# Graph network on one core: TensorE takes each batch's first product one batch earlier, ahead of the second group of sums

## The chip, the cores and the metric

The kernel runs on one core of one Trainium2 chip. The metric is device microseconds of one execution of the whole program. Ten executions of the kernel before took a median of 3623.09 us, with a lowest of 3620.8 and a highest of 3625.99.

## The reference

There are 6250 nodes with 16 features each and 200000 edges, sorted by destination. Two graph layers follow one another, each with a residual and a layer norm. The change touches only the second:

```python
w_m = (efeat @ W_msg + b_msg).reshape(E, in_f, -1)       # 16 x 16 per edge
w_a = (efeat @ W_attn + b_attn).reshape(E, in_f, -1)
h_src = feat[src][:, :, None]
e1 = w_m * h_src
e2 = w_a * h_src
seg_max = jax.ops.segment_max(e2, dst, num_segments=N)
ex = jnp.exp(e2 - seg_max[dst])
denom = jax.ops.segment_sum(ex, dst, num_segments=N)
attn = ex / denom[dst]
ft = jax.ops.segment_sum(e1 * attn, dst, num_segments=N)
return ft.sum(axis=1)
```

For every edge, then, two 16 x 16 matrices come out of a small product with the edge's 16 attributes; both are multiplied by the source node's features; one goes through a softmax over all edges of the same destination; and the other, weighted by it, is summed by destination.

## The kernel before

**First layer and node update.** Up to about 1620 us the kernel works through the first layer's edges and updates the nodes (lines up to 556). The change leaves that part as it is.

**Second layer.** The edges are cut into four stretches, and a batch takes 256 edges of each: `u` from 0 to 3 names the stretch, 128 edges in two columns. There are `NQ` = 197 batches. Inside `tc.manual_schedule(engines=ORDERED)` the instructions of TensorE, VectorE, ScalarE and GpSimd stand in each engine's queue exactly in the order in which the Python code issues them, and every engine works its queue in order. An instruction that waits holds up all that is behind it on its engine. SyncE's queue is not in `ORDERED`.

The steps of batch `b`, each a helper in the code:

- `gather(b)` (L584): GpSimd issues eight indirect DMAs, one of 128 rows each, which fetch the source nodes' features into `hb`. It is called two batches ahead (`LEAD` = 2).
- `load(b)` (L597): two DMAs from SyncE's queue bring the edge attributes into one of four buffers `ev`.
- `multiply(b, u)` (L611): four TensorE matmuls, attributes by weights, into a PSUM tile `pw`: a half for attention, a half for the message. The pool `psw` has three such tiles, used in turn. Counted through all batches, product number n takes the tile of product n - 3, and so waits until that one's last reader is done.
- `maxima(b, u)` (L623, VectorE): the attention half times the node features, to `xs`, and the largest value by row to `cm`.
- `exps(b, u)` (L629, ScalarE): the exponential of that, in place, less a reference value `neg`.
- `message(b, u)` (L634, VectorE): the message half times the node features, in place in PSUM.
- `product(b, u)` (L638, VectorE): message times exponential, to `xs`. It is the last reader of the tile `pw`.
- `highest`, `across`, `top`, `spread`, `refer` (L653, L656, L662 and L664, L667, L671): the batch's largest value is carried over the partitions by a TensorE transpose, a VectorE reduction, a TensorE matmul with a row of ones and a ScalarE copy, all through one PSUM tile `bank`, to serve as the reference of a later batch.
- `add(b, 0)` and `add(b, 1)` (L688): the two groups of sums by destination, each four matmuls with the 0/1 matrix `oh` into the single PSUM tile `acc`. They are issued in the turn of batch `b + 1`. The second group begins with one matmul (L686) that carries over the sums of the batch before.
- `leave(b)` (L694, ScalarE) copies the finished `acc` to `sums`; `invert(b)` (L699, L700) takes logarithm and exponential of it and writes to `bank`; `fold(b)` (L705, L707, VectorE) multiplies and reduces; and SyncE's queue writes the rows out (L713). They are issued in the turn of batch `b + 2`.

Because TensorE's queue is in order, its work in the turn of batch `b` before the change was: product 0, `across`, products 1 and 2, the first group of sums, `spread`, product 3, the second group of sums. On VectorE the turn runs: `maxima` 0, `message` 0, `maxima` 1, `top`, `message` 1, `product` 0, `maxima` 2, `message` 2, `product` 1, `maxima` 3, `message` 3, `product` 2, `fold`, `highest`, `product` 3. On ScalarE: `leave`, `exps` 0, `invert`, `exps` 1, three of the eight steps of `hot`, `exps` 2, `refer`, `carry`, three steps of `hot`, `exps` 3, the rest of `hot`. In the turns of batches 12, 14 and 16 VectorE also has a check of the input's order and range behind its own work.

Of the kernel before, what the change touches and what calls it, by code (L numbers as in the profile page):

```python
# [43 lines left out]
def gnn_kernel(ctx, tc, x_q, x_t4, src_p, dst_p, src_w, dst_w, prev_w, dst_r, base_h, src_q, dst_q, base_q, ea8_w, ea16, ea16_t,  # L44
# [5 lines left out]
    NQ = base_q.shape[1] // S  # L50
# [67 lines left out]
    with ExitStack() as l0:  # L118
# [166 lines left out]
        def message(b):  # L285
            v = got[b]
            pr = wp.tile([W, G, 16, 8], F32, name="pr")
            nc.vector.tensor_tensor(pr, v["pm"].rearrange("p t (h j) -> p t h j", j=8),
                                    v["ea"].unsqueeze(2).to_broadcast([W, G, 16, 8]), OP.mult)
            v["ms"] = wp.tile([W, G, 16], F32, name="ms")  # L290
            nc.vector.tensor_reduce(v["ms"], pr, AX.X, OP.add)
# [267 lines left out]
    with ExitStack() as l1:  # L559
# [17 lines left out]
        def gather(b):  # L577

            st[b] = {"hb": []}
            for u in range(G // 2):  # L580
                hb = hp.tile([W, 2, D], F32, name="hb")
                for k in range(2):
                    t = b * G + 2 * u + k
                    nc.gpsimd.indirect_dma_start(  # L584
                        out=hb[:, k, :], out_offset=None, in_=x1_dram[:, :],
                        in_offset=bass.IndirectOffsetOnAxis(ap=srcq[:, t:t + 1], axis=0))
                st[b]["hb"].append(hb)

        def load(b):
            ev = evs[b % 4]  # L590
            if b < NQ - 1:
                part = eas_dram.rearrange("r (s n) -> r s n", s=S)[:, :, b * 2 * W:(b + 1) * 2 * W]
            else:
                part = eas_dram[:, EP // S:].rearrange("r (s n) -> r s n", s=S - 1)[:, :, 0:2 * W]
            for r in (0, 32):
                to = ev[r:r + 32, :].bitcast(F32)
                nc.sync.dma_start(out=to.rearrange("r (s n) -> r s n", s=S)[:, 0:part.shape[1], :], in_=part)  # L597
                if b == NQ - 1:
                    nc.sync.dma_start(out=to[:, (S - 1) * 2 * W:], in_=end_dram)
            st[b]["ev"] = ev  # L600
            st[b]["xs"] = xp.tile([W, S, 2, 2, 256], F32, name="xs")
            st.pop(b - 6, None)

        def multiply(b, u):

            v = st[b]
            v[u] = pw = psw.tile([W, 2, 2, 256], F32, name="pw")
            for c in range(2):
                for k in range(2):
                    t = 2 * u + k  # L610
                    nc.tensor.matmul(pw[:, c, k, :], v["ev"][:, t * W:(t + 1) * W], w1[:, c * 256:(c + 1) * 256],  # L611
                                     start=True, stop=True)
# [7 lines left out]
        def maxima(b, u):  # L620

            v = st[b]
            nc.vector.tensor_tensor_reduce(  # L623
                over(v["xs"][:, u, 0]), over(v[u][:, 0]), rows(b, u),
                1.0, -2.0 * BIG, OP.mult, OP.max, cm[:, b * S + u:b * S + u + 1])

        def exps(b, u):
            x = st[b]["xs"][:, u, 0]
            nc.scalar.activation(x, x, AF.Exp, bias=neg[:, b:b + 1])  # L629
# [6 lines left out]
        def product(b, u):  # L636
            x = st[b]["xs"]
            nc.vector.tensor_tensor(x[:, u, 1], st[b][u][:, 1], x[:, u, 0], OP.mult)  # L638
# [12 lines left out]
        def highest(b):  # L651
            st[b]["m1"] = wp.tile([W, 1], F32, name="m1")
            nc.vector.tensor_reduce(st[b]["m1"], cm[:, b * S:(b + 1) * S], AX.X, OP.max)  # L653

        def across(b):
            nc.tensor.transpose(bank[0:1, 0:W], st[b]["m1"], ident)  # L656

        def top(b):

            before = st[b - 1]["top"] if b > 0 else None  # L660
            st[b]["top"] = wp.tile([1, 1], F32, name="top")
            nc.vector.tensor_reduce(st[b]["top"], bank[0:1, 0:W], AX.X, OP.max)  # L662
            if before is not None:
                nc.vector.tensor_tensor(st[b]["top"], st[b]["top"], before, OP.max)  # L664

        def spread(b):
            nc.tensor.matmul(bank[:, W:W + 1], ones_row, st[b]["top"], start=True, stop=True)  # L667

        def refer(b):

            nc.scalar.activation(neg[:, b:b + 1], bank[:, W:W + 1], AF.Copy, scale=-1.0)  # L671
# [8 lines left out]
        def add(b, k):  # L680

            v = st[b]
            if k == 0:
                v["acc"] = pss.tile([W, 512], F32, name="acc")
            elif b > 0:
                nc.tensor.matmul(v["acc"], cols[b % 3], st[b - 1]["sums"], start=False, stop=False)  # L686
            for s in range(S):
                nc.tensor.matmul(v["acc"][s * R:(s + 1) * R, :], v["oh"][:, 2 * s + k, :], v["xs"][:, s, :, k, :],  # L688
                                 start=k == 0, stop=k == 1)

        def leave(b):
            v = st[b]
            v["sums"] = wp.tile([W, 512], F32, name="sums")
            nc.scalar.activation(v["sums"], v["acc"], AF.Copy)  # L694

        def invert(b):
            v = st[b]
            r = wp.tile([W, 256], F32, name="r")
            nc.scalar.activation(r, v["sums"][:, 0:256], AF.Ln, bias=tiny_t)  # L699
            nc.scalar.activation(bank[:, 256:512], r, AF.Exp, scale=-1.0, accum_out=rsum[:, b:b + 1])  # L700
# [40 lines left out]
        with tc.issue_after(tables.ins):  # L741
            for b in range(LEAD):
                gather(b)
            load(0)
            with tc.manual_schedule(engines=ORDERED):
                for u in range(4):
                    multiply(0, u)
                    maxima(0, u)
                highest(0)
                across(0)  # L750
                top(0)
                spread(0)
                refer(0)
                refer(1)
                for b in range(NQ + 2):
                    new, old, gone = b < NQ, 1 <= b <= NQ, b >= 2
                    trail = old and b + 1 < NQ
                    if b + LEAD < NQ:
                        gather(b + LEAD)
                    if b + 1 < NQ:  # L760
                        load(b + 1)
                    if new:
                        multiply(b, 0)
                    if gone:
                        leave(b - 2)
                    if trail:
                        across(b - 1)
                    if new:
                        maxima(b, 0)
                        exps(b, 0)  # L770
                        message(b, 0)
                        multiply(b, 1)
                    if gone:
                        invert(b - 2)
                    if new:
                        maxima(b, 1)
                        exps(b, 1)
                    if trail:
                        top(b - 1)
                    if new:  # L780
                        message(b, 1)
                        multiply(b, 2)
                        product(b, 0)
                    if old:
                        add(b - 1, 0)
                    if trail:
                        spread(b - 1)
                    if new:
                        hot(b, 0, 3)
                        maxima(b, 2)  # L790
                        exps(b, 2)
                        message(b, 2)
                        product(b, 1)
                        multiply(b, 3)
                    if trail:
                        refer(b + 1)
                    if b + 1 < NQ:
                        carry(b + 1)
                    if new:
                        hot(b, 3, 6)  # L800
                        maxima(b, 3)
                        exps(b, 3)
                        message(b, 3)
                        product(b, 2)
                        hot(b, 6, G)
                    if old:
                        add(b - 1, 1)
                    if gone:
                        fold(b - 2)
                    if new:  # L810
                        highest(b)
                        product(b, 3)
                    if b in checks:
                        checks[b]()
                    if b == NQ:
                        clear()
                        far_off()
# [370 lines left out]
```

## Time and profile before

| | |
|---|---|
| median of ten executions | 3623.09 us |
| the profiled execution's own time | 3621.96 us |
| its span, first to last instruction | 3620.2 us |
| instructions | 58991 |
| busy: PE, DVE, ACT, POOL | 3169.0, 3259.6, 2789.5, 1879.7 us |
| second layer, first to last `highest` (L653) | 1620.2 to 3586.2 us |
| first and last gather issued (L584) | 1608.0 and 3579.0 us |
| mean granted TensorE clock over the execution | 0.772 |

PE is TensorE, DVE VectorE, ACT ScalarE, POOL GpSimd and SPq SyncE's DMA queue. A row of the profile names a line, an engine, an operation and `out<-in` by tile names. PEclk is the share of full clock that TensorE was granted. A matmul of 32-bit floats can be shown as two instructions. In the timeline a row gives the start, the length, and in brackets the idle time of that engine just before with what ended it.

### The profile page before, as it was taken

What the parts mean: (1) busy time and instruction counts of PE and PEld (TensorE: products, weight loads), DVE (VectorE), ACT (ScalarE), POOL (GpSimd) and SP (SyncE); (2) the same over time, 40 slices, a digit from 0 to 9 for tenths busy, and PEclk for the clock granted to TensorE, in tenths of its full rate; (3) what the DMA queues carried; (4) which work ended last, traced back from release to release, by engine and by line L of the source; (5) the groups of instructions that cost most, each with busy time, mean ns of one, the idle gap of its engine ahead of it and who ended that gap; (6) DMA issues with size and microseconds to landing.
All of it is one profiled execution on the core that took longest, in us unless ns stands there. A gap on an engine that the chain in (4) does not pass through costs nothing.

```text
span 3620.2 us, 58991 instructions
## 1 busy us (share of the span) xinstructions
PE 3169.0 (88%) x15309; PEld 2221.5 (61%) x15309; DVE 3259.6 (90%) x6470; ACT 2789.5 (77%) x5393; POOL 1879.7 (52%) x1790
## 2 busy tenths in 40 slices
PE   3999999999999999948799999999998998888896
PEld 3999999999999998834344444444444444344343
DVE  5999999999999999879999999999998899898887
ACT  4999999999999999817677777677777676677664
POOL 0222222222222222317777777777777777777774
PEclk9999999999999999956666556666666567766655
DMA  6333333333333333221111111111111111111111
GB/s 182 132 123 123 114 123 119 122 114 123 123 119 118 123 123 118 99 55 37 31 35 35 35 36 36 34 35 35 35 36 36 34 36 35 35 35 35 34 35 25
DMA packets 272706, 263.36 MB, mean 73 GB/s; under 512 B 94437, under 2 KB 233254, under 8 KB 272363
## 3 DMA queue, kind: packets, MB, share of 16 engines
q1 hardware_dynamic: 220187, 240.08, 21.4%
q0 software_dynamic: 50432, 13.01, 3.5%
q10 hardware_dynamic: 1744, 6.41, 0.6%
q8 instruction: 128, 2.10, 0.2%
q14 instruction: 215, 1.76, 0.2%
HBM read 222.08 MB, written 37.05 MB: 72 GB/s over the span
## 4 chain that ended last, share of the span: by engine, by line
PE 51%; DVE 18%; ACT 16%; issue 8%; DMA 6%; POOL 1%; SPq 0%; DVEq 0%; ACTq 0%; POOLq 0%
PE acc L348 20%; PE pw L611 11%; PE acc L688 10%; ACT away L306 6%; DVE xs L638 5%; ACT oba L308 5%; PE acc L686 5%; DVE xs L623 4%; PE pm L283 3%; DMA ev<-eas_dram 3%; DVE pw L634 2%; ACT bank L700 2%; ACT r L699 1%; DMA hb<-x_dram,srcq 1%; PE bank L667 1%
## 5 line engine op out<-in xcount | busy, mean ns | idle before, releaser
L584 POOL DMA_INDIRECT hb<-x_dram,srcq x1576 | 1491.8, 947 | 554.8 <-issue 270.7
L329 POOL TENSOR_TENSOR ll<-oa,sl 128x1024 fp32r<-128x1024 f32 x196 | 380.0, 1939 | 1144.5 <-DVE sl L336 1088.8
L629 ACT ACTIVATE xs<-xs,neg 128x512 f32<-128x512 f32 x788 | 562.9, 714 | 487.6 <-DVE cm L623 486.1
L611 PEld LDWEIGHTS pw<-w,ev 66*128 66x128 f32 x3168 | 613.3, 274 | 408.2 <-issue 300.5
L611 PE MATMUL pw<-w,ev 66*128 66x256 f32 x3168 | 742.1, 391 | 91.0 <-DVE xs L638 71.8
L306 ACT ACTIVATE away<-iota,nsb 128x784 f32<-128x784 f32 x784 | 699.2, 939 | 6.0 <-DVE nsb L184 0.6
L688 PE MATMUL acc<-xs,oh 128*32 128x512 f32 x3152 | 671.4, 939 | 0.7 <-ACT sums L694 0.7
L623 DVE CUSTOM_DVE_ANT_1 xs<-pw,hb 128x512 f32<-128x512 f32 x792 | 537.9, 679 | 88.8 <-PE pw L611 65.1
L308 ACT ACTIVATE oba<-away,one_t 128x3136 fp32r<-128x3136 f32 x196 | 572.8, 2922 | 6.4
L634 DVE TENSOR_TENSOR pw<-pw,hb 128x512 f32<-128x512 f32 x788 | 547.0, 694 | 20.5
L638 DVE TENSOR_TENSOR xs<-pw,xs 128x512 f32<-128x512 f32 x788 | 533.3, 677 | 0.0
L316 DVE TENSOR_SCALAR obd<-iota,sb 128x784 fp32r<-128x784 f32 x784 | 454.6, 622 | 0.0
L646 ACT ACTIVATE away<-iota,nrw 128x32 f32<-128x32 f32 x1576 | 389.6, 306 | 0.0
L348 PE MATMUL acc<-obd,ll 128*128 128x392 f32 x1568 | 347.5, 367 | 0.0
L686 PE MATMUL acc<-sums,col 128*128 128x512 f32 x392 | 329.7, 939 | 0.0
L348 PE MATMUL acc<-oba,ll 128*128 128x392 f32 x1568 | 325.9, 352 | 0.0
L348 PE MATMUL acc<-obd,lh 128*128 128x392 f32 x1568 | 312.8, 341 | 1.0 <-DVE lh L329 1.0
L283 PE MATMUL pm<-tw,ot 128*128 128x128 f32 x1568 | 215.0, 282 | 112.0 <-issue 89.0
L348 PE MATMUL acc<-oba,lh 128*128 128x392 f32 x1568 | 312.9, 341 | 0.0
L667 PEld LDWEIGHTS bank<-top,ones_row 1*128 1x128 f32 x392 | 84.0, 265 | 357.4 <-ACT xs L629 215.0
L348 PEld LDWEIGHTS acc<-oba,ll 128*128 128x128 f32 x1568 | 298.7, 198 | 0.0
L283 PEld LDWEIGHTS pm<-tw,ot 128*128 128x128 f32 x1568 | 207.3, 200 | 138.8 <-issue 135.1
(149 smaller groups left out, 3558.8 us busy)
## 6 DMA issues: line engine op xcount, KB each, us to landing
db<-in_dst_r SPq DMA_DIRECT2D x196, 512.0 KB
ev<-eas_dram SPq DMA_DIRECT2D x392, 128.0 KB
hb<-x_dram,srcq POOLq DMA_INDIRECT x1576
tw<-xw_dram SPq DMA_DIRECT2D x784, 32.0 KB
er<-in_ea_t SPq DMA_DIRECT2D x28, 448.0 KB
eas_dram<-eh SPq DMA_DIRECT2D x28, 448.0 KB
eas_dram<-el SPq DMA_DIRECT2D x28, 448.0 KB
tab_dram<-ft SPq DMA_DIRECT2D x784, 2.0 KB
```

The source lines that it names most:

```text
L283: nc.tensor.matmul(pm[:, t, :], v["ot"][:, t, :], v["tw"][:, 2 * t // G, :], start=True, stop=True)
L306: nc.scalar.activation(v["away"][:, t, :], iota, AF.Abs, bias=nsb[:, b * G + t:b * G + t + 1])
L308: nc.scalar.activation(v["oba"], v["away"], AF.Relu, bias=one_t, scale=-1.0)
L348: nc.tensor.matmul(acc[:, s, :B // 2], l[:, t].rearrange("p a h -> p (a h)"), ob[:, s * B // 2:(s + 1) * B // 2], start=b == 0 and t == GA ...
L584: nc.gpsimd.indirect_dma_start(out=hb[:, k, :], out_offset=None, in_=x1_dram[:, :], in_offset=bass.IndirectOffsetOnAxis(ap=srcq[:, t:t + 1 ...
L611: nc.tensor.matmul(pw[:, c, k, :], v["ev"][:, t * W:(t + 1) * W], w1[:, c * 256:(c + 1) * 256], start=True, stop=True)
L623: nc.vector.tensor_tensor_reduce(over(v["xs"][:, u, 0]), over(v[u][:, 0]), rows(b, u), 1.0, -2.0 * BIG, OP.mult, OP.max, cm[:, b * S + u:b ...
L629: nc.scalar.activation(x, x, AF.Exp, bias=neg[:, b:b + 1])
L634: nc.vector.tensor_tensor(m, m, rows(b, u), OP.mult)
L638: nc.vector.tensor_tensor(x[:, u, 1], st[b][u][:, 1], x[:, u, 0], OP.mult)
L686: nc.tensor.matmul(v["acc"], cols[b % 3], st[b - 1]["sums"], start=False, stop=False)
L688: nc.tensor.matmul(v["acc"][s * R:(s + 1) * R, :], v["oh"][:, 2 * s + k, :], v["xs"][:, s, :, k, :], start=k == 0, stop=k == 1)
```

## The change

TensorE's products are moved. Product 0 of batch `b + 1` is issued in the turn of batch `b`, right after product 3 of `b` and in front of the second group of sums. Product 1 takes the place that product 0 had at the start of the turn, and product 2 stands alone between `across` and the first group of sums. Batch 0 issues its own product 0 at the start. Nothing else is moved, and no instruction is added or taken away; the order on VectorE, ScalarE, GpSimd and SyncE's queue stays as it was.

```diff
                     if b + 1 < NQ:
                         load(b + 1)
+                    if b == 0:
+                        multiply(0, 0)
                     if new:
-                        multiply(b, 0)
+                        multiply(b, 1)
                     if gone:
                         leave(b - 2)
                     if trail:
                         across(b - 1)
                     if new:
                         maxima(b, 0)
                         exps(b, 0)
                         message(b, 0)
-                        multiply(b, 1)
...
                         product(b, 1)
                         multiply(b, 3)
+                    if b + 1 < NQ:
+                        multiply(b + 1, 0)
                     if trail:
                         refer(b + 1)
```

TensorE's work in a turn is then: product 1, `across`, product 2, the first group of sums, `spread`, product 3, product 0 of the next batch, the second group of sums.

## The prediction

> **What bounds the kernel now.** The page first. The changed lines lie in the second layer, the right half of the slices, where the clock falls to 5 to 7 tenths and the chain that ended last is mostly TensorE.
>
> ```profile
> PEclk9999999999999999956666556666666567766655
> PE 51%; DVE 18%; ACT 16%; issue 8%; DMA 6%; POOL 1%; SPq 0%; DVEq 0%; ACTq 0%; POOLq 0%
> L584 POOL DMA_INDIRECT hb<-x_dram,srcq x1576 | 1491.8, 947 | 554.8 <-issue 270.7
> ```
>
> The third line is a second bound that the chain hides: 947 ns and 0.30 us between two issues make 1.25 us, eight times a batch 10.0 us. The loop takes 1966.0 us for 197 batches (L653, 1620.2 to 3586.2), 9.98 us each. In GpSimd's timeline the gathers follow each other from 1608.0 to 3579.0 with only some 4.5 us of longer gaps, at the check batches. The loop cannot outrun them.
>
> Next the distance from each L653 to the next. Two lengths recur, 10.19 and 9.47 us; between 1825.8 and 3005.9 the mean is 9.92, a mix of 62 to 38. In a 10.19 us batch the chain of waits is TensorE alone:
>
> ```profile
> 2414.62 0.51 PE bank L667 x2
> 2415.13 1.16 PE pw L611 x4
> 2416.29 1.71 PE acc L686 x2
> 2418.00 1.87 PE acc L688 x8
> 2419.86 1.15 PE pw L611 x4
> 2421.02 0.21 PE bank L656
> 2421.23 1.71 PE pw L611 x8
> 2422.94 1.87 PE acc L688 x8
> ```
>
> These eight sum to 10.19: `spread`, product 3, second group (two lines), product 0, `across`, products 1 and 2, first group. In a 9.47 us batch the second group is about 1 us per line instead of 1.8, TensorE waits, and VectorE is full but for 0.40 us before `top`. What separates the two is the clock. The busy time in stretches of 3.413 us, laid where the clock switches, shows how it is granted (it switches only at multiples of 3.413 us):
>
> ```profile
> 2455.82:2459.23 3.41, 3.41 (x11) 1.56 (x14) 3.34 (x8) 2.81 (x10) 2.50 (x3) 0.50 0.22 49
> 2459.23:2462.65 3.42, 3.34 (x29) 1.79 (x21) 3.35 (x9) 2.15 (x6) 2.81 (x3) 1.00 0.21 44
> 2462.65:2466.06 3.41, 1.48 (x11) 1.04 (x8) 2.94 (x9) 2.29 (x8) 2.50 (x4) 1.00 0.09 8
> 2466.06:2469.47 3.41, 3.41 (x11) 0.28 (x10) 3.34 (x8) 3.31 (x11) 2.50 (x4) 0.50 0.28 82
> 2472.89:2476.30 3.41, 1.84 (x8) 1.07 (x8) 3.22 (x8) 2.29 (x8) 2.72 (x3) 1.00 0.10 15
> ```
>
> After length, columns 2 to 6 are PE, PEld, DVE, ACT, POOL busy; then the clock. A stretch full of TensorE work without `spread` or `across` (2455.82, 2466.06) is followed by full clock; one half empty (1.48 or 1.84 of 3.41) by half clock. Full stretches that hold a `spread` or an `across` stay at half (2452.41 to 2455.82 does, with `spread` at 2455.31).
>
> **The change part by part.**
>
> *TensorE's work.* The same 4 products, 8 sums, 1 carry, `across` and `spread` per batch: 10.19 us at half clock, no gain.
>
> *Removed.* `maxima` 0 no longer waits for product 0: the 0.64 us before L623 in half-clock batches goes. VectorE had that slack under TensorE's 10.19, so nothing is gained by it; `top` still waits for L700.
>
> *Products 1 and 2.* Product 1 needs `product` 2 of the batch before, ended 2418.81, a microsecond before TensorE gets there: 0. Product 2 now follows `across` directly and needs `product` 3 (starts 0.07 after `highest`, lasts 0.68). At half clock product 1 and `across` cover it (1.15 + 0.21). At full clock it waits some 0.3 us, under the 1.09 us for which `spread` waits anyway. Without that cover it would be 0.3 us a batch.
>
> *Product 0 earlier.* Its `ev` buffer was filled long before: the refill is issued at 2406.13, just as product 3 of the batch that used it ends, and there are four buffers. Cost 0. No queue of SyncE or GpSimd is passed.
>
> *The added wait.* Product 0 of the next batch is fourth after product 1 of this one, so it waits for `product` 1 on VectorE. Behind it in TensorE's queue stands the second group; for that waits `leave`, behind it on ScalarE `exps` 0 and `invert`, and for L700 waits `top`, ahead of everything that leads to `product` 1. That is a ring. Before, the second group stood behind product 3, which needs only `product` 0, 1.91 us earlier (2414.29 against 2416.20). The rows of the ring at half clock:
>
> ```profile
> 2409.74 0.60 ACT L694 ACTIVATE sums<-acc 128x512 f32<-128x512 f32 x1 [0.69 <-PE acc L688]
> 2411.60 0.72 ACT L629 ACTIVATE xs<-xs,neg 128x512 f32<-128x512 f32 x1 [1.26 <-DVE cm L623]
> 2412.23 0.49 ACT L699 ACTIVATE r<-sums,tiny_t 128x256 f32<-128x256 f32 x1
> 2412.75 0.39 ACT L700 ACTIVATE bank<-r 128x256 f32<-128x256 f32 x1
> 2413.30 0.28 DVE L662 TENSOR_REDUCE top<-bank 1x1 f32<-1x128 f32 x1 [0.40 <-ACT bank L700]
> 2416.20 0.68 DVE L638 TENSOR_TENSOR xs<-pw,xs 128x512 f32<-128x512 f32 x1
> ```
>
> Start to start: second group to L694 2.00 (2417.93 to 2419.93); L694 to `exps` 0, if that need not wait, 0.51 to 0.60 (overlapped or not); to L699 0.63; to L700 0.52; to `top` 0.55; to `product` 1 2.90; its length 0.68; to a matmul that waited for it 0.15 (2465.19 to 2465.34); product 0 before L686 0.99 (2415.10 to 2416.09); L686 before L688 1.84. Sum 10.77 to 10.86: **10.8 us** at half clock against TensorE's 10.19; before, 1.91 shorter, the ring was hidden under these. At full clock the TensorE terms shrink to about 1.05, 0.55 and 0.96, and the ring is 8.6, under VectorE's 9.47: no change there.
>
> *How often each clock.* This the trace before cannot show for the new order; bounds are all full clock (the gathers' 10.0 a batch) and all half clock (10.8). Between them: at half clock the clean run without `spread` or `across` is product 0, second group, product 1, again 1.15 + 1.71 + 1.87 + 1.16 = 5.89 us, so a 3.41 us stretch fits inside for about 2.5 of 3.41 positions. Before, 10.19 is nearly three stretches (10.24): the position moved 0.05 a batch, and a bad one lasted 58 us. At 10.8 it moves 0.56, and a bad one is passed in two or three batches. At 9.47 it moves 0.77 the other way, and full clock soon ends: in the batch around 2473 the first group ends at 2472.53 and `product` 1 starts at 2475.91, so the waited-for product 0 would start at 2475.91 + 0.68 + 0.15 = 2476.74, and TensorE has 0.35 + 0.71 us of work in those 4.2. The two drifts balance where the mean is three stretches, 10.24 us, with 0.77 / (0.56 + 0.77) = 58% long batches. With the old 62% it would be 10.30. I take 10.24, the nearest to the switching rows.
>
> *Against a page's rule.* The Trainium skill, "TensorE: Matmul & The Clock Gate", Part 1 and "HAM oscillation", says that only gaps beyond about 3 us in TensorE's work make the clock fall. Here it fell after stretches with 1.48 and 1.84 us of work, none with such a gap. By the page the full clock would hold, and the time would be the gathers', about 3623.
>
> **The sum.** 197 x 10.24 = 2017.3. The three check batches (14.87, 13.99, 13.24) are VectorE's and stay: 42.1 - 3 x 10.24 = +11.4. The first two (9.95, 7.88) stay: -2.6. Together 2026.1 against 1966.0: +60. The span goes from 3620.2 to 3680; the profiled execution's 3621.96 is 1.1 below the median of 3623.09, so I forecast 3683.
>
> **The rivals.** *Not slower: the gathers still decide.* If half-clock batches fall below (10.01 - 9.47) / (10.8 - 9.47) = 41%, the ring hides under 10.0 us of gathers. For it: the faster drift. Against: the emptier full-clock batch. Time 3618 to 3626; it can gain no more than the 4.5 us of gaps, so a gain beyond 0.2% (7.2 us, about what can be measured) is almost excluded. Chance 0.10, and 0.03 for a real gain.
>
> *The wait is hidden, and the change does nothing.* VectorE, freed of 0.64 us, runs ahead, and `product` 1 is done when TensorE arrives. That needs the ring to be 0.6 us shorter than its rows; `top` behind L700 speaks against it. Time 3623, chance 0.05.
>
> *Half clock throughout.* With an idle gap in each batch, full stretches become rare. 197 x (10.8 - 10.24) = 110 more: 3793. Against: the clean run is as long as before. Chance 0.06.
>
> **The numbers.** Forecast 0.76, its own range 3655 (mean 10.10) to 3712 (10.39). For 8 in 10 the low end must reach into the two unchanged cases: 3624 to 3712. Faster 0.03, same 0.14, slower 0.83.
>
> **What would show it.** Right: rows of L611 with an idle of about 0.6 us <-L638 just before L686; `leave` later; L653 distances of 9.5 and 10.7 to 10.9, mean near 10.24; gathers with gaps that VectorE ends. Wrong: distances of 10.19 still there (no ring), a mean of 10.0 with gathers back to back (gathers decide), or a clock of 0.5 throughout.

## The result, and the profile after

The changed kernel takes 3680.41 us (median of 8 runs, 3679.17 to 3681.66), the kernel before, beside it, 3622.31 us: a ratio of 1.0159, with an interval of 1.015 to 1.0168. It is 58 us slower. The profiled execution has a span of 3677.1 us. From the first to the last `highest` (L653) it takes 1619.1 to 3642.0, that is 2022.9 us, where it took 1966.0.

First the page: the clock, the shares of the chain that ended last, and two groups (instructions and their busy time and mean, then the idle time before them and what ended most of it).

```profile
PEclk9999999999999999857777777777777777777776
ACT 39%; PE 26%; DVE 17%; issue 10%; DMA 7%; POOL 0%; SPq 0%; DVEq 0%; ACTq 0%; POOLq 0%
L623 DVE CUSTOM_DVE_ANT_1 xs<-pw,hb 128x512 f32<-128x512 f32 x792 | 538.2, 680 | 146.2 <-PE pw L611 137.2
L694 ACT ACTIVATE sums<-acc 128x512 f32<-128x512 f32 x197 | 117.7, 597 | 344.9 <-PE acc L688 344.9
```

Before the change the group of `leave` read:

```profile
L694 ACT ACTIVATE sums<-acc 128x512 f32<-128x512 f32 x197 | 116.5, 591 | 76.8 <-PE acc L688 72.3 <-issue 2.1
```

The granted clock has risen from 5 to 7 tenths to a steady 7, while the kernel has become slower. The shares of the chain must not be read as a picture of the second layer: they cover the whole execution. ScalarE's rise from 16% to 39% is mostly the first layer's (L306 and L308, 6% and 5% before, 17% and 13% now), and TensorE's fall from 51% to 26% is mostly the 20% that it had there before, at L348. The change leaves these lines as they are; the chain only takes another way through them. For the same reason the 51% before do not say that TensorE bounds the second layer; the rows of one batch do that. The last line is of the second layer: `leave` waited 72.3 us in all for the second group of sums, and waits 344.9 now. That is the wait which the prediction foretold, not the price of it.

Next the chain of waits through one long batch (start, length, engine, tile and line).

```profile
2410.90 1.19 PE pw L611 x4
2412.09 1.71 PE acc L686 x2
2413.80 1.91 PE acc L688 x8
...
2415.73 0.60 ACT sums L694
2416.33 0.61 ACT xs L629
2416.94 0.41 ACT r L699
...
2417.37 0.52 ACT bank L700 x2
...
2417.91 0.29 DVE top L662
```

This is the ring that the prediction wrote down: product 0 of the next batch, the carry, the second group, `leave`, `exps` 0, `invert`, `top`. From `top` it goes on over VectorE's turn to `product` 1 at 2420.82, and from there to the next product 0 at 2421.60. In the timeline of the same batch (start, length, then in brackets the idle time before and what ended it) the joints can be read:

```profile
2410.12 0.68 DVE L638 TENSOR_TENSOR xs<-pw,xs 128x512 f32<-128x512 f32 x1
2410.90 1.19 PE L611 MATMUL pw<-w,ev 66*128 66x256 f32 x4 [1.25 <-issue]
2415.73 0.60 ACT L694 ACTIVATE sums<-acc 128x512 f32<-128x512 f32 x1 [2.57 <-PE acc L688]
2416.86 0.69 DVE L623 CUSTOM_DVE_ANT_1 xs<-pw,hb 128x512 f32<-128x512 f32 x1 [1.18 <-PE pw L611]
```

Product 0 starts 0.10 us after the end of `product` 1 (2410.12 + 0.68 = 2410.80); the profile puts its 1.25 us of idle time down to "issue", but that is the instant at which its tile came free. `leave` then waits 2.57 us. In the fourth row `maxima` 1 waits 1.18 us for product 1, which now stands where product 0 stood.

From batch 20 on, the 177 distances from one L653 to the next are 9.46 us (65 of them) and 10.64 to 10.75 us (109, mean 10.70); the length of 10.19 is gone. The mean is 10.23; before it was 9.95 over the same batches.

What separates the two lengths is the clock under a part of the ring, from the start of product 0 to the start of `leave`. Two such stretches, one of a short batch and one of a long (window, its length, busy PE, PEld, DVE, ACT, POOL with their counts, clock, DMA share, GB/s):

```profile
2401.44:2404.08 2.64, 2.64 (x15) 1.04 (x16) 2.57 (x6) 2.24 (x9) 1.89 (x2) 1.00 0.39 106
2410.90:2415.73 4.83, 4.83 (x15) 1.66 (x15) 4.67 (x11) 2.23 (x8) 3.61 (x5) 0.50 0.24 64
```

Taken from each product 0 to the next, from batch 21 on, all 109 long distances had this stretch wholly at half clock, and all 64 short ones had it wholly at full clock.

### The profile page after: what moved, and what is told of

Same layout as the page of the kernel before. It is cut to its first block, busy times and chain, and to the rows that moved or that the text cites. A ratio compares the mean times of both kernels' runs of the same rounds, so it can differ in the third digit from the quotient of the medians.

```text
span 3677.1 us, 58991 instructions
## 1 busy us (share of the span) xinstructions
PE 3015.1 (82%) x15309; PEld 2143.9 (58%) x15309; DVE 3260.3 (89%) x6470; ACT 2780.2 (76%) x5393; POOL 1880.2 (51%) x1790
## 4 chain that ended last, share of the span: by engine, by line
ACT 39%; PE 26%; DVE 17%; issue 10%; DMA 7%; POOL 0%; SPq 0%; DVEq 0%; ACTq 0%; POOLq 0%
ACT away L306 17%; ACT oba L308 13%; PE pw L611 11%; PE acc L688 8%; PE acc L686 6%; DVE xs L638 5%; DMA ev<-eas_dram 5%; DVE pw L634 3%; ACT bank L700 2%; ACT r L699 2%; DVE xs L623 1%; DVE top L662 1%; ACT sm L296 1%; ACT xs L629 1%; ACT sums L694 1%
## 5 line engine op out<-in xcount | busy, mean ns | idle before, releaser
L611 PE MATMUL pw<-w,ev 66*128 66x256 f32 x3168 | 722.9, 368 | 345.8 <-issue 186.4
L611 PEld LDWEIGHTS pw<-w,ev 66*128 66x128 f32 x3168 | 565.2, 248 | 697.3 <-issue 483.3
L306 ACT ACTIVATE away<-iota,nsb 128x784 f32<-128x784 f32 x784 | 699.2, 939 | 5.9 <-DVE nsb L184 0.5
L623 DVE CUSTOM_DVE_ANT_1 xs<-pw,hb 128x512 f32<-128x512 f32 x792 | 538.2, 680 | 146.2 <-PE pw L611 137.2
L308 ACT ACTIVATE oba<-away,one_t 128x3136 fp32r<-128x3136 f32 x196 | 572.7, 2922 | 6.4
L688 PE MATMUL acc<-xs,oh 128*32 128x512 f32 x3152 | 567.3, 801 | 0.7 <-ACT sums L694 0.7
L634 DVE TENSOR_TENSOR pw<-pw,hb 128x512 f32<-128x512 f32 x788 | 547.0, 694 | 20.5
L638 DVE TENSOR_TENSOR xs<-pw,xs 128x512 f32<-128x512 f32 x788 | 533.4, 677 | 0.0
L694 ACT ACTIVATE sums<-acc 128x512 f32<-128x512 f32 x197 | 117.7, 597 | 344.9 <-PE acc L688 344.9
L348 PE MATMUL acc<-obd,ll 128*128 128x392 f32 x1568 | 346.8, 366 | 0.0
L348 PE MATMUL acc<-oba,ll 128*128 128x392 f32 x1568 | 325.9, 352 | 0.0
L348 PE MATMUL acc<-obd,lh 128*128 128x392 f32 x1568 | 312.7, 341 | 1.0 <-DVE lh L329 1.0
L348 PE MATMUL acc<-oba,lh 128*128 128x392 f32 x1568 | 312.8, 341 | 0.0
L686 PE MATMUL acc<-sums,col 128*128 128x512 f32 x392 | 309.6, 885 | 0.0
L348 PEld LDWEIGHTS acc<-oba,ll 128*128 128x128 f32 x1568 | 298.8, 198 | 0.0
L348 PEld LDWEIGHTS acc<-obd,ll 128*128 128x128 f32 x1568 | 291.3, 202 | 0.0
```

The lines of the kernel that those rows point to most:

```text
L306: nc.scalar.activation(v["away"][:, t, :], iota, AF.Abs, bias=nsb[:, b * G + t:b * G + t + 1])
L308: nc.scalar.activation(v["oba"], v["away"], AF.Relu, bias=one_t, scale=-1.0)
L348: nc.tensor.matmul(acc[:, s, :B // 2], l[:, t].rearrange("p a h -> p (a h)"), ob[:, s * B // 2:(s + 1) * B // 2], start=b == 0 and t == GA ...
L623: nc.vector.tensor_tensor_reduce(over(v["xs"][:, u, 0]), over(v[u][:, 0]), rows(b, u), 1.0, -2.0 * BIG, OP.mult, OP.max, cm[:, b * S + u:b ...
L634: nc.vector.tensor_tensor(m, m, rows(b, u), OP.mult)
```

## The experiments

### Where the loss sits: three positions of one product, and a longer ring

The theory: the whole loss is the ring, closed by product 0 of the next batch standing ahead of the carry and the second group. The rival: products 1 and 2, each moved a step, cost something too. A second question was the prediction's way of getting a mean, which says that short and long batches balance at three clock stretches (10.24 us) whatever the ring's length.

**Product 0 behind the second group**, all else as in the changed kernel:

```diff
-                    if b + 1 < NQ:
-                        multiply(b + 1, 0)
                     if trail:
                         refer(b + 1)
...
                     if old:
                         add(b - 1, 1)
+                    if b + 1 < NQ:
+                        multiply(b + 1, 0)
```

> The changed order, but product 0 of the next batch is issued behind the second group of sums instead of in front of it; products 1 and 2 stay where the change put them. Ring theory (the second group stands behind a product that waits for `product` 1, and so the chain over ScalarE and VectorE closes at 10.8 us at half clock): the ring loses the wait and 0.99 us, half-clock batches are TensorE's 10.19 us again, the gathers bound the loop, 3617 to 3627 us. Rival, the two products that were taken one step sooner (product 2 now waits for the last `product` of the batch before): nothing changes, 3675 to 3685 us.

It took 3621.43 us, a ratio to the kernel before of 1.0001 (0.9991 to 1.0011). The distances are mostly 9.46 to 9.5 and 10.19 again, and `leave` waits about as little as before the change:

```profile
L694 ACT ACTIVATE sums<-acc 128x512 f32<-128x512 f32 x197 | 116.7, 592 | 87.7 <-PE acc L688 84.3 <-issue 0.7
```

Products 1 and 2 a step sooner therefore cost nothing here. Whether they bring a little cannot be seen in the time, because the gathers' 10.0 us a batch would hide it. The rival falls.

**Product 0 alone**: the kernel before, with only product 0 of the next batch in front of the second group.

```diff
-                    if new:
-                        multiply(b, 0)
+                    if b == 0:
+                        multiply(0, 0)
...
+                    if b + 1 < NQ:
+                        multiply(b + 1, 0)
                     if trail:
                         refer(b + 1)
```

> The order before, and only product 0 of the next batch moved in front of the second group; products 1 and 2 stay behind `across` together. Ring theory: the whole loss is there, 3670 to 3690 us, with batches of 9.46 and about 10.7 us. Rival, products 1 and 2 one step sooner: no loss, 3617 to 3627 us.

It took 3683.38 us, 1.0174 (1.0157 to 1.0191): the whole loss comes with this one product. Its group of `leave`, to be read against the changed kernel's:

```profile
L694 ACT ACTIVATE sums<-acc 128x512 f32<-128x512 f32 x197 | 117.6, 597 | 416.0 <-PE acc L688 416.0
```

Long batches are 10.70 us again (83 of them). The others lie between 9.6 and 10.06 instead of at 9.46, and the mean is 10.24. In these others the stretch from product 0 to `leave` was at half clock for 67 to 82% of its time, and no batch had it wholly at full clock; they too are the ring, with the clock changing under it. That the sum of the two kinds comes out as in the changed kernel is not explained by any run.

**Product 0 between the carry and the sums.** One step later than in the changed kernel: the carry (L686) goes first, then product 0, then the four sums. In `add`, behind the carry's matmul:

```diff
+            if k == 1 and b + 2 < NQ:
+                multiply(b + 2, 0)
...
-                    if b + 1 < NQ:
-                        multiply(b + 1, 0)
+                    if b == 0:
+                        multiply(1, 0)
```

> The changed order, but product 0 of the next batch is issued between the matmul of the carry (L686) and the four of the second group, so it still stands in front of the sums. Ring theory: the 1.84 us of the carry now run beside the wait and leave the ring, which falls to 10.8 - 1.84 = about 9.0 us, below TensorE's 10.19; 3617 to 3627 us, and no idle time of TensorE before product 0 at half clock. Rival, that any product in front of the four sums delays `leave` too much (its 0.99 us, not the wait): still 3660 us or more.

It took 3621.21 us, 1.0001 (0.9991 to 1.001): no loss. TensorE's timeline shows why:

```profile
2412.00 1.23 PE L611 MATMUL pw<-w,ev 66*128 66x256 f32 x4
2413.02 1.91 PE L686 MATMUL acc<-sums,col 128*128 128x512 f32 x2
2414.25 1.53 PE L611 MATMUL pw<-w,ev 66*128 66x256 f32 x4
```

The first line is product 3, the third is product 0, and no bracket of idle time stands behind either. The carry's time at half clock covers the wait for `product` 1 (which ended at 2414.15). The ring is still closed, but it is shorter by the carry's step, 1.84 us, and so falls under TensorE's 10.19 again. The distances are spread from 9.46 to about 10.3, with a mean of 9.96. `leave` still waits 200.3 us in all for the second group, and the time shows none of it.

**A ring 0.31 us longer**: the changed kernel with the reduction of `top` (L662) issued twice.

```diff
             nc.vector.tensor_reduce(st[b]["top"], bank[0:1, 0:W], AX.X, OP.max)
+            nc.vector.tensor_reduce(st[b]["top"], bank[0:1, 0:W], AX.X, OP.max)
```

> The changed order with the reduction of `top` (L662) done twice, 0.31 us more on VectorE in every batch, on the ring and on VectorE's own sum. Theory that the batches lock to three clock windows of 3.413 us: lengths become 9.77 and about 11.0 us, long ones get rarer, the mean stays at 10.24 to 10.32, 3675 to 3695 us. Rival, no lock, the share of long batches stays near what it is: 197 x 0.31 = 61 us more, 3735 to 3745 us.

It took 3730.06 us, 1.0298 (1.0281 to 1.0315). That is 49.65 us more than the changed kernel, 0.25 a batch for 0.31 us of work; it lies far above the range for the balance and 5 us below the range of its rival. In the profiled execution, the slowest of the four, the mean is 10.50 us a batch. The long batches, 56 of them, take 11.0 us, which is 10.70 + 0.31: that is what a ring does. The mean goes against the prediction's balance, by which it would have stayed at 10.24. Some 120 batches lie from 9.9 to 10.5, and none at 9.77 (9.46 + 0.31). Those had half clock for 66 to 82% of the stretch from product 0 to `leave`; none had full clock throughout.

### Are the gathers a bound?

The prediction called the gathers a second bound that the loop cannot outrun. So half of them were taken out.

```diff
+        hbs = [keep.tile([W, 2, D], F32, name=f"hb{k}") for k in range(LEAD * G // 2)]
+        for hb in hbs:
+            nc.gpsimd.memset(hb, 1.0)
...
-                hb = hp.tile([W, 2, D], F32, name="hb")
-                for k in range(2):
+                hb = hbs[(b * (G // 2) + u) % len(hbs)]
+                for k in range(1):
```

In the kernel before:

> The order before with only one of every two gathers issued (the second half of every node tile is a constant, so the messages of those edges are not the reference's): GpSimd needs 5 us a batch instead of 10. If the gathers only cut off the last quarter of the loop, the mean batch goes from 9.98 to the 9.92 of the part without gather waits: 3608 to 3618 us. If they are what bounds the whole loop, as the prediction said, more than that comes free: below 3605 us.

In the changed kernel:

> The changed order with only one of every two gathers issued, as in the run beside it. Ring theory: the gathers run far ahead and bound nothing, 3675 to 3685 us, the same batch lengths. Rival, that the slower loop comes from gathers that wait longer for their tiles: below 3660 us.

They took 3626.23 us and 3685.01 us. They ran on another chip, on which the kernel before, with all its gathers, took 4246.53 us (see the last section), so their ratios to it say nothing; their batches can be compared, since with half the gathers TensorE and VectorE keep their pace there too (9.46 and 10.19 us in the one, 9.46, 10.64 and 10.75 in the other). In the kernel before, the first two batches take 10.8 us longer with the preset tiles; without them the loop is 1942.6 us against 1948.2, so that 788 gathers less give back 5.6 us. Without those 10.8 us, 3626.23 would lie in the range of the theory that the gathers only cut off the last quarter. The place fits it too: from batch 20 to 139 the mean is 9.91 with all the gathers and with half, and over the last 49 batches 10.03 with all and 9.86 with half. In the changed kernel the mean stays 10.23. So the gathers were a bound before, but only once the lead that they start with was used up, and they held hardly more than that last quarter.

### Two more changes to the ring, which tell nothing

`leave` lengthened by two tiny ScalarE copies (some 0.3 us), and `invert` put ahead of `exps` 0, which takes `exps` 0 out of the ring; each run twice, on two chips.

```diff
+            for _ in range(2):
+                idle = wp.tile([W, 1], F32, name="idle")
+                nc.scalar.activation(idle, eps_t, AF.Copy)
```

```diff
+                    if gone:
+                        invert(b - 2)
                     if new:
                         maxima(b, 0)
                         exps(b, 0)
...
-                    if gone:
-                        invert(b - 2)
```

> The changed order with two tiny ScalarE copies behind `leave`, some 0.37 us more on the ring and nowhere else (ScalarE has idle time, VectorE and TensorE get no work). Ring without a lock: the long batches, 62% of them, grow to about 11.07 us, 0.37 x 0.62 x 197 = 45 us more, about 3725 us. Lock to three clock windows: long batches get rarer, mean still 10.24 to 10.28, 3680 to 3690 us. Rival, the ring does not run over `leave`: no change of any length, 3680 us with long batches still 10.7.

> The changed order with `invert` right behind `leave` on ScalarE, ahead of `exps` 0 instead of behind it: the ring's leg over ScalarE loses 0.63 us, and the leg over product 1 and `maxima` 1 becomes the longer one; long batches 10.40 us. Without a lock: 0.3 x 0.62 x 197 = 37 us less, about 3643 us. With the lock to three windows: the mean stays at 10.24, 3675 to 3685 us. Rival, the ring does not run over `leave` and `invert`: long batches still 10.7, 3680 us.

> The kernel of the longer `leave` once more (two tiny ScalarE copies behind `leave`, some 0.3 us more on the ring and nowhere else). Ring without a lock: the 62% long batches grow from 10.7 to about 11.0 us, 0.3 x 0.62 x 197 = 37 us more, about 3717 us. Lock to three clock windows: mean still 10.24 to 10.28, 3680 to 3690 us. Rival, the ring does not run over `leave`: long batches still 10.7, 3680 us.

> The kernel with `invert` ahead of `exps` 0 on ScalarE once more. Without a lock: long batches 10.40 us, about 3643 us. With the lock: the mean stays at 10.24, 3675 to 3685 us. Rival, the ring does not run over `leave` and `invert`: long batches still 10.7, 3680 us.

They took 4309.36 and 4297.82 us beside a kernel before of 4246.53, and 4329.69 and 4311.97 beside one of 4263.95. The waits of the third (engine, tile and line, what was waited for: sum, times, longest) show what decided there:

```profile
POOL hb L584 <- DVE pw L634: 772.6, 253, 6.1
DVE xs L623 <- remote: 583.2, 132, 7.4
```

GpSimd waits for VectorE to free the buffers, and `maxima` waits, for something the profile only calls remote, 583.2 us in all; in the kernel before on its usual chip `maxima` waited 22.8 us for its gathers. The mean batch is 13.4 to 13.6 us. On these same two chips kernels with half the gathers run at 9.6 to 10.2 us a batch, so the gathers set the pace here and not the ring. The changed kernel itself, with all its gathers, was not run there, so there is also no time to compare with. All four are inconclusive; the ring was lengthened only at `top`.

### Does the clock's fall make the long batches?

The prediction took half clock to follow from stretches in which TensorE has little to do. If so, useless work in TensorE's gaps should hold the clock up and make the loop faster; the rival is that extra matmuls in front of the waiting product only lengthen the ring. Product 3 and the first group of sums are each issued three times, into the same places.

```diff
+            for _ in range(3 if u == 3 else 1):
...
-            for s in range(S):
+            for n in range(3 if k == 0 else 1):
+                for s in range(S):
...
-                                 start=k == 0, stop=k == 1)
+                                 start=k == 0, stop=k == 1 or n < 2)
```

In the changed kernel, and in the one with half the gathers:

> The changed order with useless work for TensorE in its gaps: product 3 and the first group of sums are each issued three times over, the repeats overwriting the same values; 3.0 us more of TensorE work a batch at full clock, 5.6 at half. Clock theory (a 3.413 us window that is half empty ends full clock, and only half clock makes the ring longer than VectorE's 9.47 us): no window is half empty any more, the clock stays full, the ring is 8.6 us, and the loop goes back to the pace of the gathers: 3617 to 3630 us, granted clock near 1 in the loop. Rival, the clock does not follow TensorE's gaps: the extra work comes on top at half clock, over 15 us a batch, 4000 us or more.

> The filled kernel of the run beside it with only one of every two gathers issued (so the messages of half the edges are not the reference's). If the filled loop is held by the gathers alone, it falls to VectorE's 9.47 us a batch: 0.5 x 197 = 100 us less than with all gathers, about 3520 us. If something else holds it at 10.0, the time stays at 3617 to 3630 us.

The first took 4436.48 us on a chip with late gathers (a mean of 13.99 us a batch) and is inconclusive. The second took 3575.2 us. Against the same kernel without the extra work, 3685.01 us, which leaves out the same gathers but ran on another chip, that is 110 us less, with about 2.7 us more of TensorE work at full clock in every batch (the first group takes 2.78 us instead of 1.06, product 3 1.68 instead of 0.73). One stretch of the loop in both, the kernel without the extra work first (window, its length, busy PE, PEld, DVE, ACT, POOL with their counts, clock, DMA share, GB/s):

```profile
1840.00:3560.00 1720.00, 1362.62 (x6219) 655.44 (x6218) 1506.82 (x3530) 1170.07 (x3365) 634.40 (x673) 0.75 0.13 31
```

```profile
1840.00:3560.00 1720.00, 1591.95 (x10829) 794.90 (x10825) 1589.74 (x3737) 1246.24 (x3546) 652.58 (x693) 0.97 0.14 33
```

The clock goes from 0.75 to 0.97, VectorE from 1506.8 to 1589.7 us busy of 1720. Of 177 batches 145 take about 9.46 us, VectorE's length, and 29 about 10.3. The expectation, near 3520, was that all would be short; about every sixth batch still lost the clock, and the first two batches alone take 15 us more than in the kernel before. That the long batches of the changed kernel come from the fall of the clock is shown by this together with the clock under each batch (above): where the clock is held up, most of them go. Whether this version would beat the kernel before with all its gathers is open: with them it ran only where the gathers land late, and elsewhere their 10.0 us a batch would stand above 9.46.

## Why the prediction was right, and where it was not

*The added wait: right.* Measured in the batch shown, start to start: product 0 to the carry 0.99 us, to the sums 1.84, to `leave` 2.00, to `exps` 0 0.50, to L699 0.61, to L700 0.53, to `top` 0.54, to `product` 1 2.91, and 0.78 from there to the next product 0. That is 10.70, where the rows of before gave 10.77 to 10.86. At full clock the batch has VectorE's length, as said: 9.46.

*Products 1 and 2, and the earlier `ev`: right, at nothing.* Product 0 behind the second group leaves 3621.43 us, with the gathers as a floor.

*The sum: right.* The loop grew by 56.9 us; forecast were 60. The check batches take 14.87, 13.98 and 13.12 us, with 14.87, 13.99 and 13.24 before.

*How often each clock: right in size here, wrong as a rule.* The long batches are 62% and not 58%. Put into the prediction's own balance, the measured lengths give 0.78 / (0.46 + 0.78) = 63%, and 0.62 x 10.70 + 0.38 x 9.46 = 10.23. But with 0.31 us more in the ring the mean went to 10.50, so nothing holds it at three clock stretches. The forecast is this balance times 197, so that it came within 3 us is in part luck, as far as the runs show. Why the changed kernel, product 0 alone, and the changed kernel with half its gathers all end at 10.23 to 10.24 is open.

*What makes the clock fall: right for this kernel, too simple as a rule.* The changed kernel's clock stretches around the batch shown:

```profile
2406.67:2410.09 3.42, 1.13 (x10) 0.82 (x6) 2.95 (x9) 2.33 (x7) 2.75 (x3) 1.00 0.07 8
2410.09:2413.50 3.41, 2.60 (x6) 1.35 (x6) 3.34 (x8) 2.97 (x11) 2.56 (x3) 0.50 0.31 89
2413.50:2416.91 3.41, 3.41 (x15) 1.43 (x15) 2.19 (x7) 1.18 (x3) 2.50 (x4) 0.50 0.08 8
2416.91:2420.33 3.42, 2.65 (x19) 1.38 (x18) 3.00 (x9) 2.31 (x9) 2.51 (x3) 1.00 0.07 7
```

After 1.13 us of work in 3.42, with no gap of 3 us in it, two stretches at half clock follow, and after a full one the clock is back. Between 1700 and 3500 us all 70 full-clock stretches of this kernel with less than 2.0 of 3.41 us of TensorE work were followed by half clock, and of the 199 with more only 7. The Trainium skill, "TensorE: Matmul & The Clock Gate", gives as the abstract rule in "HAM oscillation" that there be no idle gaps of TensorE beyond about 3.4 us. Here the clock fell without one.

But "half empty" is not the whole condition. In the run with the extra work and half the gathers:

```profile
2784.81:2788.22 3.41, 2.92 (x23) 2.41 (x20) 3.34 (x9) 2.26 (x10) 1.89 (x2) 1.00 0.05 5
2788.22:2791.64 3.42, 3.42 (x11) 0.39 (x9) 3.39 (x8) 1.61 (x5) 0.95 (x1) 0.50 0.29 82
```

The clock fell after 2.92 us of work in 3.41. Of the 31 falls between 1700 and 3500 us in that run 28 were of this kind, while other stretches as full kept the clock; why is open. Nor does a full stretch with a piece of `across` always stay at half: the one at 2413.50 above holds the start of `across` (2416.62), and full clock follows.

*The removed wait: the place was wrong, the price was right.* The 0.64 us of `maxima` 0 did not go; VectorE now waits at `maxima` 1 for product 1 instead. In all, `maxima` waits 137.2 us for products where it waited 65.1. Since the ring decides, that costs nothing of its own.

*The gathers as a bound that the loop cannot outrun: right as a sum, of little weight.* With half of them away the kernel before came from 9.95 to 9.90 us a batch, so its own pace lies hardly below their 10.0, and they hold it only in the last quarter. The changed kernel, at 10.23, is above their pace.

*The signs.* The distances were as given. The idle time before product 0 is 1.25 us under "issue" and not 0.6 under L638, because product 3 had run early at full clock. The gaps between gathers that VectorE ends are there (112.1 us behind L634).

*The rivals.* The hidden wait and the half clock throughout did not happen: `leave` waits, and the clock is 0.75 in the stretch from 1840 to 3560, where it was 0.63. The gathers do not decide.

## What to carry to other kernels

In a queue worked in order, a matmul that must wait, put ahead of one that need not, joins two chains, and they may close into a ring through the other engines: write it down start to start, once for each clock, and compare it with what the engines take for themselves. A single step can decide: in front of the carry the product cost 1.6%, behind it nothing. A second resource whose pace nearly equals the loop's may hold only a part of it; the lead that it keeps, or taking half of it away, tells how much. And the shares of a chain over the whole execution can shift in a part that was not changed: read the waits of the changed lines.

## What the runs showed of the hardware that was not expected

A higher clock went with a slower kernel (0.63 to 0.75, and 58 us more): what counted was the clock under product 0, the carry and the second group, half in all 109 long batches and full in all 64 short ones. Why half clock filled less of the loop as a whole was not tried. And useless work made a loop faster: 3575.2 us with product 3 and the first group issued three times, 3685.01 without, both with half the gathers, on two chips.

On two other chips the gathers held the loop, it seems by landing late. GpSimd's own time for each was the same, 0.944 us, but `maxima`, which waited there, started about 22 us after its gather's issue had ended, where in the kernel before on its usual chip it was as little as 1.4 us, and the kernel before took 4246.53 and 4263.95 us instead of 3621. With 16 gathers for two batches of 13.4 us, that is 1.68 us for each. Why was not tried.
